# One of sixteen weight transfers of a pair issued from GpSimd's queue instead of SyncE's, in a cross-attention block

## The chip, the cores and the metric

The kernel runs on one core of a Trainium2 chip. The metric is the device time of one execution in microseconds, and less is better. A core has five engines that run side by side and wait for one another by semaphores: TensorE (PE, with PEld for its weight loads), VectorE (DVE), ScalarE (ACT), GpSimd (POOL) and SyncE (SP). Each takes its instructions in the order in which the program issues them. A DMA is issued from the queue of one engine, and its bytes are moved by 16 DMA engines that all queues share. In this kernel nearly all DMAs are issued from SP.

## The reference

A transformer block on 128 sequences of 128 tokens and 256 features, all in float32, with 16 heads of 16 features each and a hidden layer of 1024:

```python
q = (query @ Wq + bq).reshape(b, s, N_HEADS, D_K).transpose(0, 2, 1, 3)
k = (key @ Wk + bk).reshape(b, s, N_HEADS, D_K).transpose(0, 2, 1, 3)
v = (values @ Wv + bv).reshape(b, s, N_HEADS, D_K).transpose(0, 2, 1, 3)
scores = jnp.einsum('bhqd,bhkd->bhqk', q, k) / jnp.sqrt(jnp.float32(D_K))
allowed = j < i + mask                      # mask is 0: strictly earlier tokens
scores = jnp.where(allowed, scores, NEG_INF)
attn = jax.nn.softmax(scores, axis=-1)
attn = attn.at[:, :, 0, :].set(0.0)
ctx = jnp.einsum('bhqk,bhkd->bhqd', attn, v)
ctx = ctx.transpose(0, 2, 1, 3).reshape(b, s, d)
x = layer_norm(query + ctx @ Wo + bo, ln1_g, ln1_b)
ffn = jax.nn.relu(x @ W1 + b1) @ W2 + b2
out = layer_norm(x + ffn, ln2_g, ln2_b)
```

`query` is the input `x`, `key` and `values` are the input `ctx_1024`.

## The kernel before

**Pairs and steps.** Two sequences form a pair, so there are 64 pairs. The schedule is written out by hand: for every engine, the order of the calls in the program is the order in which that engine works. Pairs 0 to 8 and 61 to 63 have their calls written out one by one. In between, `steps(9, 60)` runs one list, `order`, once per step. An entry of that list is a name and a lag, and `ops` says what the name does for which pair, so that one step holds the scores of pair p, the softmax weighting of pair p - 1 (`weigh`, lag -1 on `p - 2`), the hidden layer of pair p - 3 and the second product of pair p - 4.

**What happens to the attention weights.** For pair p the scores come from TensorE (`scores_both`, L502), are masked by VectorE (L516, L974), turned into exponentials by ScalarE (L997) and multiplied by the reciprocal of their sums by GpSimd (`sums`, L557, three calls a pair). VectorE then transposes them within blocks of 32 x 32 (`turn`, L574, three calls a pair), from `sm` into `tb`. The blocks now stand on the wrong partitions. `bring` (L600) carries them to the right ones: 16 DMAs, SBUF to SBUF, one for each row block i and each block column j, from 32 partitions of `tb` to 32 partitions of `pT`, 768 floats on each. `EVERY` is `range(16)`, and `u` = 4 i + j. The DMAs are issued at L608, in four groups of four: `br0`, `br4`, `br8`, `br12` (L1488 to L1491). One step later `weigh` multiplies `pT` with the values (L642, L652). `sm`, `tb` and `pT` rotate through four buffers (`wide`), and the buffer of `pT` for pair p is that of `tb` for pair p - 1.

**The order at the end of a step.** These are the last entries of `order`, with the engine that each one uses:

| Entry | What it issues | Engine |
|---|---|---|
| `sum0` | third `sums` of pair p (L557) | GpSimd |
| `bo` | adds a bias to the tokens (L274) | GpSimd |
| `turn2` | third `turn` of pair p (L574) | VectorE |
| `fin1` | half of the last layer norm of pair p - 5 (L787, L794) | ScalarE, GpSimd |
| `x1g` | scales a residual of pair p - 3 (L761) | GpSimd |
| `x1out` | four DMAs of the first layer norm's result to DRAM (L256) | SP |
| `br0` | four DMAs of `bring` | SP |
| `x1in` | one DMA back from DRAM (L262) | SP |
| `br12`, `br4`, `br8` | twelve DMAs of `bring` | SP |

The next step's first GpSimd instruction is `hs2` (L1025). With `hs0` (L1023), `hs1` (L1027) and `hs3` (L1029) it combines the hidden layer of a pair into `hS`, from which the second product (L1064, `S3` to `S7`) reads. The calls `xs0` to `xs3` (L1110 to L1116) do the same for the hidden layer's input, `xS`, read by L1156. L717 to L724 work out the scale and shift of both layer norms (`sd`, `nb`), which ScalarE reads at L745 and L787.

GpSimd issues no DMA in this kernel.

Of the kernel before, what the change touches and what calls it, by code (L numbers as in the profile page):

```python
# [20 lines left out]
def tile_cross_attention_block(  # L21
# [22 lines left out]
    nc = tc.nc  # L44
# [401 lines left out]
    def wide(name):  # L446
        kind, p = name.split("_")
        turn_ = 3 * (int(p) - 7) + ("sm", "tb", "pT").index(kind)
        at = SOFT[name] if name in SOFT else (2, 3, 1, 0)[turn_ % 4]
        return soft.tile([P, NS * (H + HH) * 32], F32, tag=f"wide{at}", name=name)  # L450
# [149 lines left out]
    def bring(p, queue, which):  # L600

        st = states[p]
        if "pT" not in st:
            pT = st["pT whole"] = wide(f"pT_{p}").rearrange("p (i n) -> p i n", i=NS)
            st["pT"] = pT.rearrange("p i (n a) -> p i n a", a=32)
        for u in which:
            i, j = u // NS, u % NS
            queue.dma_start(  # L608
                st["pT whole"][32 * j : 32 * j + 32, i, :], st["tb"][32 * i : 32 * i + 32, j, :]
            )  # L610
# [665 lines left out]
    EVERY = range(NS * NS)  # L1276
# [81 lines left out]
    def step_tables():  # L1358
# [129 lines left out]
            "br0": lambda p: bring(p, nc.sync, EVERY[0:4]),  # L1488
            "br4": lambda p: bring(p, nc.sync, EVERY[4:8]),
            "br8": lambda p: bring(p, nc.sync, EVERY[8:12]),  # L1490
            "br12": lambda p: bring(p, nc.sync, EVERY[12:16]),  # L1491
        }
        order = (
# [20 lines left out]
        return ops, order  # L1514

    ops, order = step_tables()

    def steps(first, last):
# [1432 lines left out]
```

## Time and profile before

| What | Value |
|---|---|
| Median of two runs | 1477.27 us (1477.25 to 1477.29) |
| Profiled execution, from its first to its last instruction | 1476.5 us |
| Mean granted clock of TensorE | 0.999 |
| DMAs of `bring` (L608), all from SP | 976, of 96 KB each |
| Bytes moved on SP's queue (q1) | 202.49 MB |

A row of a group of instructions names its line, engine, operation and what is written from what is read, then the shapes, the count, the busy time in us, the mean of one in ns, and the idle time of the engine just before them with what ended it. A row of the timeline gives start and length in us. A row of waits gives the sum in us, how often, and the longest. The busy times of a stretch list, for each engine, busy us and the number of instructions, then TensorE's granted clock, the share of the DMA engines that was in use, and GB/s. SPq, POOLq and PEldq are the queues of these engines: DMA issues and semaphore instructions, which the profile does not count as the engine's busy time.

### The profile page before, as it was taken

The numbers are of one execution on the slowest core, as the hardware profiler recorded it, in microseconds if no ns is written. First come the engines' busy times: TensorE is split into PE (matmuls) and PEld (weight loads), VectorE is DVE, ScalarE is ACT, GpSimd is POOL, SyncE is SP. The second block draws the span as 40 slices with busy tenths as digits, with TensorE's granted clock in tenths as the row PEclk, the third lists the DMA queues.
The fourth block names the chain that finished last, engine by engine and source line by source line (L and its number), as shares of the span: only waits on it lengthen the run. The fifth ranks groups of instructions, "written<-read, shape, count | busy, mean of one in ns | idle before, by whom it ended". The sixth has DMA issues, their size and how long they took to land.

```text
span 1476.5 us, 53972 instructions
## 1 busy us (share of the span) xinstructions
PE 1463.9 (99%) x19696; PEld 1377.8 (93%) x19696; DVE 1315.5 (89%) x2897; ACT 1323.0 (90%) x5279; POOL 1388.2 (94%) x1484
## 2 busy tenths in 40 slices
PE   9999999999999999999999999999999999999998
PEld 7788999999999999999999999999999999999998
DVE  7999899999998998998998999989989999999866
ACT  5758999999999999999999999999999999999863
POOL 7788999999999999999999999999999999999987
PEclk9999999999999999999999999999999999999999
DMA  8465566655656666666556566556565666664451
GB/s 203 96 141 127 133 146 139 147 138 136 156 141 138 141 146 139 148 144 145 138 135 154 139 142 141 144 135 157 141 139 136 146 141 150 136 152 122 116 162 58
DMA packets 417865, 206.22 MB, mean 140 GB/s; under 512 B 282434, under 2 KB 386114, under 8 KB 417602
## 3 DMA queue, kind: packets, MB, share of 16 engines
q1 hardware_dynamic: 416080, 202.49, 58.3%
q8 instruction: 159, 2.61, 0.8%
q14 instruction: 106, 0.85, 0.2%
q10 hardware_dynamic: 1520, 0.27, 0.1%
HBM read 71.84 MB, written 34.87 MB: 72 GB/s over the span
## 4 chain that ended last, share of the span: by engine, by line
PE 95%; DVE 1%; POOL 1%; DMA 1%; SPq 1%; issue 1%; ACT 0%; DVEq 0%; POOLq 0%
PE phs L1156 25%; PE pX L1064 11%; PE po L671 7%; PE pk L281 7%; PE pz L1064 7%; PE py L1064 7%; PE pv L411 7%; PE pq L351 6%; PE pss L502 6%; PE pc L652 4%; PE pc L642 3%; PE ph L917 1%; PE pq L281 1%; PE py L940 1%; SPq L608 1%; POOL sm L557 1%
## 5 line engine op out<-in xcount | busy, mean ns | idle before, releaser
L557 POOL TENSOR_TENSOR sm<-sm,rs 128x1024 f32<-128x1024 f32 x192 | 364.0, 1898 | 2.4 <-DVE rs L566 2.3
L997 ACT ACTIVATE sm<-pss,nmx 128x128 f32<-128x128 f32 x944 | 331.9, 395 | 8.4 <-DVE nmx L980 2.4
L997 ACT ACTIVATE sm<-sm,nmx 128x64 f32<-128x64 f32 x944 | 321.4, 361 | 0.8 <-DVE nmx L987 0.2
L1190 ACT ACTIVATE hT<-hT,b1e_c 128x256 f32<-128x256 f32 x480 | 216.1, 501 | 53.9 <-DVE hT L1181 44.7
L574 DVE STREAM_TRANSPOSE tb<-sm 128x1024 f32<-128x1024 f32 x186 | 227.8, 1226 | 1.5 <-POOL sm L557 1.4
L997 ACT ACTIVATION_READ_ACCUMULATOR sm<-pss,nmx 128x1 f32 x912 | 214.7, 235 | 0.0
L997 ACT ACTIVATION_READ_ACCUMULATOR sm<-sm,nmx 128x1 f32 x912 | 193.8, 212 | 0.0
L1156 PE MATMUL phs<-xS,w1t 128*128 128x128 f32 x1440 | 180.2, 275 | 0.0
L1156 PEld LDWEIGHTS phs<-xS,w1t 128*128 128x128 f32 x1440 | 170.4, 192 | 0.0
L980 DVE TENSOR_REDUCE nmx<-pss 128x4 f32<-128x512 f32 x236 | 160.6, 682 | 1.9
L401 ACT ACTIVATE kT<-pk,bkh,half 128x256 f32<-128x256 f32 x252 | 140.0, 559 | 4.1 <-PE pk L281 4.1
L516 DVE TENSOR_TENSOR sm<-pss,neg 128x256 f32<-128x256 f32 (+1 forms) x276 | 113.8, 436 | 16.5 <-PE pss L502 12.5
L1064 PE MATMUL pX<-wt,hS 128*128 128x128 f32 x960 | 126.8, 275 | 0.0
L1156 PE MATMUL phs<-x1T,w 128*128 128x128 f32 x960 | 126.5, 275 | 0.0
L1156 PEld LDWEIGHTS phs<-x1T,w 128*128 128x128 f32 x960 | 120.7, 192 | 3.0
L671 PE MATMUL po<-wo,cxT 128*128 128x256 f32 x512 | 121.8, 381 | 0.0
L411 PE MATMUL pv<-wv,cT 128*128 128x256 f32 x512 | 120.9, 379 | 0.0
L281 PE MATMUL pk<-cT,wk 128*128 128x256 f32 x504 | 119.5, 380 | 0.0
L1064 PEld LDWEIGHTS pX<-wt,hS 128*128 128x128 f32 x960 | 117.0, 192 | 0.1
L411 PEld LDWEIGHTS pv<-wv,cT 128*128 128x128 f32 x512 | 96.9, 190 | 13.1
L671 PEld LDWEIGHTS po<-wo,cxT 128*128 128x128 f32 x512 | 92.5, 190 | 12.2 <-issue 1.6
L281 PEld LDWEIGHTS pk<-cT,wk 128*128 128x128 f32 x504 | 91.5, 190 | 10.5 <-issue 0.2
(192 smaller groups left out, 4149.3 us busy)
## 6 DMA issues: line engine op xcount, KB each, us to landing
pT<-tb SPq DMA_DIRECT2D x976, 96.0 KB, 2.3
x1t<-tbx SPq DMA_DIRECT2D x252, 64.0 KB, 2.7
x1T<-x1t SPq DMA_DIRECT2D x63, 256.0 KB, 3.4
out_dram<-t SPq DMA_DIRECT2D x63, 256.0 KB, 4.3
xb<-in_x_dram SPq DMA_DIRECT2D x124, 128.0 KB, 3.3
cb<-in_ctx_dram SPq DMA_DIRECT2D x124, 128.0 KB, 3.2
x<-in_x_dram SPq DMA_DIRECT2D x31, 512.0 KB, 5.0
w<-in_L_xattn_W_dram SPq DMA_DIRECT2D x2, 1024.0 KB, 7.8
```

Of the source, the lines that this page charges most:

```text
L281: nc.tensor.matmul(ps[:, m * TP : (m + 1) * TP], w[:, k, m * P : (m + 1) * P], src[:, k, :], start=(k == 0), stop=(k == KC - 1),)
L401: nc.scalar.activation(st["kT"][:, m, e, :], pk[:, m * TP : (m + 1) * TP], AF.Identity, bias=bkh[:, m, e : e + 1], scale=half[:, e : e + 1],)
L411: nc.tensor.matmul(pv[:, s * D : (s + 1) * D], st["cT"][:, k, s * P : (s + 1) * P], wv[:, k, :], start=(k == 0), stop=(k == KC - 1),)
L516: nc.vector.tensor_tensor(probabilities(p, hi)[:, 4 * r : 4 * r + 4, :], st["sps", hi][r][:, : 4 * n].rearrange("p (n j) -> p n j", j=n), ...
L557: nc.gpsimd.tensor_tensor(sm[:, part, :], sm[:, part, :], rs[:, :, None].to_broadcast([P, part.stop - part.start, n]), ALU.mult,)
L574: nc.vector.transpose(st["tb"][:, :, at : at + 256].rearrange("p j (n a) -> p n j a", a=32), probabilities(p, hi).rearrange("p h j -> p (h ...
L671: nc.tensor.matmul(po[:, s * D : (s + 1) * D], cxT[:, k, s, :], wo[:, k, :], start=(k == 0), stop=(k == KC - 1),)
L980: nc.vector.tensor_reduce(maxima(p, 1)[:, 4 * r : 4 * r + 4], st["sps", 1][r].rearrange("p (n j) -> p n j", j=P), AX.X, ALU.max, negate=True,)
L997: nc.scalar.activation(sm[:, h, :], src, AF.Exp, bias=nmx[:, h : h + 1], scale=1.0, **({"accum_out": st["su", hi][:, h : h + 1]} if summed ...
L1064: nc.tensor.matmul(out, left(k), right(k), start=(first and k == 0), stop=(k == K - 1), skip_group_check=True,)
L1156: nc.tensor.matmul(ps[:, i * P : (i + 1) * P].rearrange("p (n a) -> p n a", a=32), left(i), right, start=(i == 0 and which not in self.ONT ...
L1190: nc.scalar.activation(self.hT[:, f], self.hT[:, f], AF.Relu, bias=b1e_c[:, f : f + 1], scale=1.0,)
```

## The change

In `br12` the first three transfers (u = 12, 13, 14) go on being issued from SP, and the fourth (u = 15, from partitions 96 to 127 of `tb` to partitions 96 to 127 of `pT`) is issued from GpSimd's queue. `br12` is called through `ops` for pairs 7 to 62. Pairs 2 to 6 call `bring` directly and stay with SP, as does pair 63, which goes by way of DRAM.

```diff
@@ -1488,7 +1488,7 @@
             "br0": lambda p: bring(p, nc.sync, EVERY[0:4]),
             "br4": lambda p: bring(p, nc.sync, EVERY[4:8]),
             "br8": lambda p: bring(p, nc.sync, EVERY[8:12]),
-            "br12": lambda p: bring(p, nc.sync, EVERY[12:16]),
+            "br12": lambda p: (bring(p, nc.sync, EVERY[12:15]), bring(p, nc.gpsimd, EVERY[15:16])),
         }
```

The function that both calls reach is not changed:

```python
for u in which:
    i, j = u // NS, u % NS
    queue.dma_start(
        st["pT whole"][32 * j : 32 * j + 32, i, :], st["tb"][32 * i : 32 * i + 32, j, :]
    )
```

Nothing else in the program differs.

## The prediction

> **What bounds the kernel now.** I read the page first, then the chain that ended last in order of time, then the busy times of single steps, then the waits and the timeline of each engine inside one step.
>
> ```profile
> PE 1463.9 (99%) x19696; PEld 1377.8 (93%) x19696; DVE 1315.5 (89%) x2897; ACT 1323.0 (90%) x5279; POOL 1388.2 (94%) x1484
> PE 95%; DVE 1%; POOL 1%; DMA 1%; SPq 1%; issue 1%; ACT 0%; DVEq 0%; POOLq 0%
> ...
> 808.21 4.47 PE phs L1156 x40
> 830.66 4.47 PE phs L1156 x40
> ```
>
> The first two lines are the page's, the other two the chain's. TensorE carries 95% of the chain, and the same forty matmuls come back after 830.66 - 808.21 = 22.45 us. That is one step, in which every pair of the pipeline advances by one stage. What the other engines have left in a step is told by the busy times of exactly one step:
>
> ```profile
> core 0: us, PE busy (x) PEld busy (x) DVE busy (x) ACT busy (x) POOL busy (x), PEclk, DMA share, GB/s
> 816.54:838.98 22.44, 22.44 (x312) 21.41 (x311) 20.42 (x48) 21.24 (x89) 21.65 (x23) 1.00 0.65 153
> ```
>
> TensorE is full, at a granted clock of 1.00. GpSimd (POOL) is busy 21.65 us of 22.44. So it is the runner-up, with 0.79 us free at most, and most of that is not free either, as its timeline shows around the place of the change:
>
> ```profile
> 810.71 1.90 POOL L557 TENSOR_TENSOR sm<-sm,rs 128x1024 f32<-128x1024 f32 x1
> 812.57 1.30 POOL L274 TENSOR_TENSOR xb<-x,bov_r 128x512 f32<-128x512 f32 x1
> 813.82 1.30 POOL L794 TENSOR_TENSOR t<-t,g_r 128x512 f32<-128x512 f32 x1
> 815.08 1.27 POOL L761 TENSOR_TENSOR t<-t,g_r 128x512 f32<-128x512 f32 x1
> 816.54 1.27 POOL L1025 TENSOR_TENSOR hS<-hT 128x512 f32<-128x512 f32 x1 [0.19 <-ACT hT L1190]
> ...
> 821.45 1.27 POOL L1027 TENSOR_TENSOR hS<-hS,hT 128x512 f32<-128x512 f32 x1
> 822.80 1.27 POOL L1029 TENSOR_TENSOR hS<-hT,hS 128x512 f32<-128x512 f32 x1
> ```
>
> Each instruction starts as the one before it ends. The exceptions are gaps of about 0.08 us before an instruction that reads its predecessor's result (L1029 after L1027, 822.80 - 822.72), which stay whatever happens, and one wait for ScalarE before L1025. The waits of GpSimd from 200 to 1340 us say how much it waits for others:
>
> ```profile
> POOL hS L1025 <- ACT hT L1190: 8.9, 50, 0.2
> POOL sd L717 <- DVE mv L1318: 1.7, 11, 0.2
> ```
>
> 8.9 / 50 = 0.18 us of true slack a step (the second row adds 0.03, and I leave it). GpSimd could run a step in 22.45 - 0.18 = 22.27 us. It is a second bound, 0.8% behind the first.
>
> **What the change does, part by part.** `br12` (L1491) is called for pairs 7 to 62, which are 56 pairs. Of its four transfers the last (u = 15: row block 3 to partitions 96 to 127, 96 KB) goes to GpSimd's queue. The transfers of pairs 2 to 6 and 63 are as before.
>
> *Taken from SyncE (SP): one issue a pair.*
>
> ```profile
> L608 SPq DMA_DIRECT2D pT<-tb x976: 507/591/2024, 55.7 to 1409.1; - x196
> ...
> DMA to landing us min/median/max: 2.0/2.3/5.5
> ...
> SPq L256 <- DVE tbx L882: 209.1, 58, 7.1
> 815.03 1.51 SPq L608 DMA_DIRECT2D pT<-tb  x1
> ...
> 819.12 8.42 SPq L608 DMA_DIRECT2D pT<-tb  x12
> ```
>
> The issue takes 591 ns (median). SP waits 209.1 / 58 = 3.6 us a step for VectorE's `tbx`, so 0.59 us less on it makes its idle longer and no more. Nor is an earlier landing worth anything. SP's last issue of the step ends at 819.12 + 8.42 = 827.54 and lands within 5.5 us, at 833.0, and the reader of these weights (`weigh`, L642) starts one step after this row:
>
> ```profile
> 812.61 0.43 PE L642 MATMUL pc<-pT,vd 128*32 128x64 f32 x16
> 813.63 1.23 DVE L574 STREAM_TRANSPOSE tb<-sm 128x1024 f32<-128x1024 f32 x1
> 824.02 1.06 PE L1064 MATMUL pX<-wt,hS 128*128 128x128 f32 x8
> ```
>
> That is at 812.61 + 22.45 = 835.06. This part I cost at nothing. Its cover is at least 2 us before the weigh and 3.6 us of idle SP.
>
> *Put on GpSimd: one issue a pair, between L761 (`x1g`) and L1025 (`hs2` of the next step).* Does it wait there? It needs the transposed weights: VectorE's L574 ends at 813.63 + 1.23 = 814.86, and GpSimd reaches the issue at 815.08 + 1.27 = 816.35, so the data has been there for 1.5 us. It also needs the old content of its target buffer read, the weights `tb` of the pair before. SP needs the same and issues from 815.03. So there is no wait, and nothing is queued up by one. The transfer itself would land by 816.35 + 2 + 5.5 = 823.9 even with a slow issue, 11 us ahead of the weigh.
>
> What remains is the time for which the issue keeps GpSimd from L1025, and the trace of before shows no DMA issued by GpSimd. Rows near it, groups of instructions with the mean in ns (those of L717 to L557 from 200 to 1340 us, the others of the whole span):
>
> ```profile
> L140 POOL MEMSET power<- 128x4 f32 x1 | 0.1, 101 | 0.3 <-POOLq L2932 0.3
> ...
> L717 POOL TENSOR_TENSOR sd<-mv,eps 128x4 f32<-128x4 f32 x51 | 10.3, 202 | 7.3 <-DVE mv L1318 1.7
> L718 POOL TENSOR_TENSOR sd<-sd,power 128x4 f32<-128x4 f32 x51 | 51.9, 1017 | 4.0
> L1029 POOL TENSOR_TENSOR hS<-hT,hS 128x512 f32<-128x512 f32 x51 | 65.0, 1274 | 4.0
> L557 POOL TENSOR_TENSOR sm<-sm,rs 128x1024 f32<-128x1024 f32 x152 | 288.4, 1897 | 0.0
> ...
> L1181 DVE TENSOR_TENSOR hT<-hT,phs 128x512 f32<-128x512 f32 x60 | 41.3, 689 | 11.1 <-PE phs L1156 10.7
> ```
>
> From below, the price is the shortest thing that GpSimd does, 0.10 us, which fits into the 0.18 us of slack. A gain is excluded, since GpSimd is only given work and SP's saving falls into idle time. From above, it is 1.90 us, GpSimd's longest instruction (SP's own longest issue of such a transfer, 2.02 us, lies close). Between these ends I take the same issue's 0.591 us on SP, times the ratio by which GpSimd is slower than another engine at a like piece of work, L1029 against VectorE's L1181: 1274 / 689 = 1.85. That is 1.09 us, an estimate. The row nearest to it points the same way: the power of four columns takes 1.02 us where an addition of the same shape takes 0.20, so an instruction that makes GpSimd work through something longer costs about a microsecond at almost no data.
>
> The Trainium skill, in "DMA: Bandwidth & Descriptors", section Specifications, gives about 1 µs to the first byte of a DMA from GpSimd, and about 0.6 µs for one from the sync queue. The second agrees with the 591 ns of the SP row here; the first no row of this trace can show. With 1.0 us for the issue the sum below would end at 1522 us.
>
> *What this does to the step.* GpSimd's step becomes 22.27 + 1.09 = 23.36 us, and TensorE's stays 22.45. GpSimd is then the bound, and falls back by 1.09 - 0.18 = 0.91 us a step until TensorE waits for it. The first of its results that TensorE misses is `hs1` (L1027, ended at 821.45 + 1.27 = 822.72), read by the matmuls at 824.02: 1.30 us of cover, used up in the second step. ScalarE feels it at once:
>
> ```profile
> ACT hT L1190 <- DVE hT L1181: 38.9, 51, 0.8
> ACT t L745 <- POOL nb L724: 18.5, 51, 0.4
> ```
>
> It already waits 18.5 / 51 = 0.36 us a step for GpSimd's `nb`, but has another 38.9 / 51 = 0.76 us of waiting ahead of the relus, and with a longer step more.
>
> *Taking the transfer on a second queue.* `weigh` has one more semaphore to look at. The nearest row for that is TensorE's own:
>
> ```profile
> L1064 PEldq EVENT_SEMAPHORE  x128: 51/51/51, 144.3 to 1461.1; - x128
> ```
>
> At worst that is 56 x 0.051 = 2.9 us. TensorE, no longer the bound, has 0.9 us a step in which it vanishes, so I count nothing. If GpSimd did not become the bound, it would be on the path.
>
> **The sum.** 56 x 0.91 = 51.0 us, less the 1.3 us of cover, is +49.7 us. The profiled execution spans 1476.5 us and the median of the two runs is 1477.27, 0.8 more. 1476.5 + 49.7 + 0.8 = 1527.0 us, which is 3.4% more.
>
> **The rivals.**
>
> *GpSimd's queue issues while its engine computes (no change).* The issue would pass beside L761's 1.27 us, as SP's issues pass beside everything. Then 0.18 us of slack is never exceeded and the time is 1477, or 1480 with the extra semaphore on TensorE. For it: a DMA issue is not an elementwise instruction, and no row shows one holding up GpSimd's engine. Against it: none shows one that doesn't, and GpSimd takes its instructions in order. The Trainium skill speaks on both sides. "DMA: Bandwidth & Descriptors", section Issuing engines are not separate DMA queues, says that issuing from several engines only saves the issuing sequencer's time, by which this change would be nearly free; "GPSIMD Engine Reference", section 4, says that the descriptors of such a DMA are made by two of GpSimd's own cores, by which it is not. No run so far shows either. Chance 10%, and another 4% for an issue that does hold the engine but costs less than SP's 0.59 us: 1477 to 1499.
>
> *A heavier issue, or a wait at it.* If the issue takes longer than 1.90 us, or has to wait on GpSimd for something that came before SP's issues, every instruction behind it waits too. SP's first issue of this step took 1.51 us where the median is 0.59, so some transfers are slow to leave. At 2.5 us: 56 x (2.5 - 0.18) - 1.3 = +129, 1606 us. Against it: the data is there 1.5 us early, and the buffer is free when SP starts. Chance 5%.
>
> *Faster.* It would take a wait of TensorE that goes. TensorE idles 1476.5 - 1463.9 = 12.6 us in all, 0.9% of the span, none of it for these weights in the steady steps. Chance 1%.
>
> **How the numbers follow.** The forecast, that GpSimd's issue costs between 0.59 and 1.90 us and GpSimd sets the step, has 80%. At 0.59 us the time is 56 x 0.41 - 1.3 = +21.7, 1499 us; at 1.90 us it is 56 x 1.72 - 1.3 = +95, 1572 us. This is the range, with 15% left out below and 5% above. The line of 2%, which is about what a measurement of this kernel can tell from no change, is at +29.5 us, an issue of (29.5 + 1.3) / 56 + 0.18 = 0.73 us. I give 6% to the stretch from 0.59 to 0.73 us. Slower by over 2%: 80 - 6 + 5 = 79%. Within 2%: 10 + 4 + 6 = 20%. Faster: 1%.
>
> **What would show it.** In the profile after: 56 issues of L608 on GpSimd's queue, and between L761 and L1025 a stretch of about 1.1 us where 0.19 us stood. The steps in the chain 23.36 us apart instead of 22.45. The wait of L1025 for ScalarE gone. TensorE waiting for `hS` or `xS` by about 0.9 us a step, and GpSimd in the chain. If the steps stay at 22.45, the issue is beside the engine's work; if they are longer than 23.4 and GpSimd still stands still ahead of the issue, it is a wait; if they are longer with GpSimd standing elsewhere, a loop through other engines set the pace and my sum by GpSimd alone was wrong.

## The result, and the profile after

The changed kernel takes 1493.53 us (median of two runs, 1492.06 to 1495.01) against 1477.27 us before. The ratio is 1.011, with a 95% interval of 1.0081 to 1.0140. It is slower by 1.1%. That is the direction of the forecast and a third of its size, and it lies under the low end of the range, 1499.

The profiled execution spans 1493.0 us, 16.5 more than that of before. On the page, the busy times and the queue of GpSimd's DMAs read as follows:

```profile
PE 1475.0 (99%) x19696; PEld 1380.5 (92%) x19696; DVE 1314.6 (88%) x2897; ACT 1325.0 (89%) x5279; POOL 1415.9 (95%) x1540
...
q0 software_dynamic: 1792, 5.51, 1.6%
...
pT<-tb POOLq DMA_DIRECT2D x56, 96.0 KB, 2.7
```

GpSimd has 56 instructions more (1540 against 1484), though only DMA issues were added to it. So the issues count as work of the engine itself, which the issues of SP do not. GpSimd's busy time grows by 1415.9 - 1388.2 = 27.7 us. The transfers land 2.7 us after the issue.

The timeline of GpSimd over the same place of a step shows the issue in its row, and the next step's L1025:

```profile
813.84 0.46 POOL L1116 TENSOR_TENSOR xS<-x1T,xS 128x128 f32<-128x128 f32 x1
814.26 0.20 POOL L717 TENSOR_TENSOR sd<-mv,eps 128x4 f32<-128x4 f32 x1
...
822.20 1.29 POOL L761 TENSOR_TENSOR t<-t,g_r 128x512 f32<-128x512 f32 x1
823.43 0.58 POOL L608 DMA_DIRECT2D pT<-tb  x1
824.04 1.28 POOL L1025 TENSOR_TENSOR hS<-hT 128x512 f32<-128x512 f32 x1
...
846.66 1.28 POOL L1025 TENSOR_TENSOR hS<-hT 128x512 f32<-128x512 f32 x1
```

The issue starts as L761 ends, takes 0.58 us, and moves L1025 to 824.04 - 823.43 = 0.61 us after its start. There is no wait ahead of L608, and L1025 no longer waits for ScalarE. The step is 846.66 - 824.04 = 22.62 us, 0.17 more than before, not 0.91 more.

The starts of L1025 also divide the 16.5 us by where they arise. The first one stands at 147.76 us before and at 149.27 after; the last one, 59 starts later, at 1458.48 and at 1472.91:

| Stretch | Before | After | Difference |
|---|---|---|---|
| Start of the span to the first L1025 | 147.76 | 149.27 | +1.5 |
| First to last L1025 | 1310.72 | 1323.64 | +12.9 |
| Last L1025 to the end | 18.02 | 20.09 | +2.1 |

56 steps at 0.18 us make 10, less than the 12.9 of the middle row. The rest shows in the later steps. These are the starts of L1025 from GpSimd's timeline between 1180 and 1310 us:

```profile
1187.28 1.28 POOL L1025 TENSOR_TENSOR hS<-hT 128x512 f32<-128x512 f32 x1
1210.43 1.28 POOL L1025 TENSOR_TENSOR hS<-hT 128x512 f32<-128x512 f32 x1
1233.06 1.28 POOL L1025 TENSOR_TENSOR hS<-hT 128x512 f32<-128x512 f32 x1
1256.19 1.28 POOL L1025 TENSOR_TENSOR hS<-hT 128x512 f32<-128x512 f32 x1
1278.84 1.28 POOL L1025 TENSOR_TENSOR hS<-hT 128x512 f32<-128x512 f32 x1
1302.11 1.28 POOL L1025 TENSOR_TENSOR hS<-hT 128x512 f32<-128x512 f32 x1
```

The distances are 23.15, 22.63, 23.13, 22.65 and 23.27 us: every second step is half a microsecond longer. Up to about 600 us all were 22.6 to 22.7; after that about every fourth is longer by 0.1 to 0.3, and from about 1140 us on every second one as here. The waits from 200 to 1340 us, and TensorE's timeline at one of the long steps, say where it stops:

```profile
ACT t L745 <- POOL nb L724: 37.7, 50, 1.1
DVE tb L574 <- POOL sm L557: 22.0, 39, 1.0
...
ACT hT L1190 <- DVE hT L1181: 20.6, 50, 0.8
...
PEld pss L502 <- issue: 8.6, 13, 1.0
PE pss L502 <- issue: 3.4, 9, 0.7
```

```profile
1230.05 1.12 PE L502 MATMUL pss<-kT,qT 32*64 32x128 f32 x34
1231.41 1.09 PE L502 MATMUL pss<-kT,qT 32*64 32x256 f32 x30 [0.24 <-issue]
```

The first two rows of the waits are GpSimd's lag, felt by the others: ScalarE waits 37.7 / 50 = 0.75 us a step for `nb` where it was 0.36, and VectorE's transposes now wait for `sums`. The last two rows are something else. TensorE stops in the midst of the 64 matmuls of the scores, and the profile names no releaser. The two rows, of its weight loads and of its matmuls, are largely the same stops. No such row stands among the waits of before. The third thing is at the very end, in the drain of GpSimd's queue (L2946; the three numbers are shortest, median and longest in ns). The first row is of before, the second of after:

```profile
L2946 POOLq DRAIN  x3: 39/78/651, 1472.5 to 1476.2; - x3
```

```profile
L2946 POOLq DRAIN  x3: 34/102/5244, 1487.0 to 1492.7; - x3
```

### The profile page after: what moved, and what is told of

Same layout as the page of the kernel before. It is cut to its first block, busy times and chain, and to the rows that moved or that the text cites. A ratio compares the mean times of both kernels' runs of the same rounds, so it can differ in the third digit from the quotient of the medians.

```text
span 1493.0 us, 54034 instructions
## 1 busy us (share of the span) xinstructions
PE 1475.0 (99%) x19696; PEld 1380.5 (92%) x19696; DVE 1314.6 (88%) x2897; ACT 1325.0 (89%) x5279; POOL 1415.9 (95%) x1540
## 5 line engine op out<-in xcount | busy, mean ns | idle before, releaser
L1190 ACT ACTIVATE hT<-hT,b1e_c 128x256 f32<-128x256 f32 x480 | 216.0, 501 | 36.0 <-DVE hT L1181 27.5
L997 ACT ACTIVATION_READ_ACCUMULATOR sm<-sm,nmx 128x1 f32 x912 | 190.7, 209 | 0.0
L1156 PE MATMUL phs<-xS,w1t 128*128 128x128 f32 x1440 | 180.8, 276 | 0.0
L1156 PEld LDWEIGHTS phs<-xS,w1t 128*128 128x128 f32 x1440 | 170.3, 192 | 0.1
L516 DVE TENSOR_TENSOR sm<-pss,neg 128x256 f32<-128x256 f32 (+1 forms) x276 | 113.9, 436 | 27.1 <-PE pss L502 23.1
L1156 PE MATMUL phs<-x1T,w 128*128 128x128 f32 x960 | 126.5, 275 | 0.0
L1156 PEld LDWEIGHTS phs<-x1T,w 128*128 128x128 f32 x960 | 120.9, 192 | 2.8
L671 PE MATMUL po<-wo,cxT 128*128 128x256 f32 x512 | 121.8, 381 | 0.0
L745 ACT ACTIVATE t<-t,nb,sd 128x256 f32<-128x256 f32 x126 | 69.4, 594 | 47.3 <-POOL nb L724 45.3
L502 PE MATMUL pss<-kT,qT 32*64 32x256 f32 (+1 forms) x3840 | 103.7, 331 | 3.6 <-issue 3.4
```

Of the source, the lines that this page charges most:

```text
L516: nc.vector.tensor_tensor(probabilities(p, hi)[:, 4 * r : 4 * r + 4, :], st["sps", hi][r][:, : 4 * n].rearrange("p (n j) -> p n j", j=n), ...
L671: nc.tensor.matmul(po[:, s * D : (s + 1) * D], cxT[:, k, s, :], wo[:, k, :], start=(k == 0), stop=(k == KC - 1),)
L997: nc.scalar.activation(sm[:, h, :], src, AF.Exp, bias=nmx[:, h : h + 1], scale=1.0, **({"accum_out": st["su", hi][:, h : h + 1]} if summed ...
L1156: nc.tensor.matmul(ps[:, i * P : (i + 1) * P].rearrange("p (n a) -> p n a", a=32), left(i), right, start=(i == 0 and which not in self.ONT ...
L1190: nc.scalar.activation(self.hT[:, f], self.hT[:, f], AF.Relu, bias=b1e_c[:, f : f + 1], scale=1.0,)
```

## The experiments

Three causes were in question: GpSimd's time for the issue, the stops of TensorE, and the drain. Each run was compared with runs of the kernel before on the same chip (medians 1476.68, 1476.94 and 1476.84 us).

The stops of TensorE need one fact. In a step of before, TensorE's queue holds exactly 640 instructions: 310 weight loads, 310 matmuls, semaphore instructions, and six empty ones which `Second(p - 4, 6)` adds. After the change it holds 639, since the number of semaphore instructions fell. The first row is of before, the second of after (instructions of the weighing, L642):

```profile
L642 PEldq EVENT_SEMAPHORE  x315: 51/51/2114, 64.9 to 1432.9; - x158
```

```profile
L642 PEldq EVENT_SEMAPHORE  x263: 51/51/1685, 66.4 to 1448.1; - x132
```

That matters if TensorE's instructions come in blocks. The page of before lists a queue for them:

```profile
q8 instruction: 159, 2.61, 0.8%
```

159 packets of 2.61 MB are 16.4 KB each, and 2.61 MB over the 40,655 instructions that the trace has for TensorE's queue are 64 bytes each: a packet is a block of 256 instructions, and 640 are two and a half blocks. At 640 a step the ends of the blocks stand at the same five places of every two steps. At 639 they move by one instruction a step. The theory was that a block whose end falls in the scores comes too late. The rival was that the stops are a consequence of GpSimd's lag.

### Filled up to 640 again (e1_pe640)

```diff
-        return once("second", p - 4, lambda: Second(p - 4, 6))
+        return once("second", p - 4, lambda: Second(p - 4, 7))
```

> The changed kernel with one more empty instruction a step on TensorE (7 pads instead of 6), so that its queue again holds 640 instructions a step as before the change, where the change had left 639. Theory T (two losses: GpSimd's step is 22.63 us, and TensorE's instruction fetch slips by one instruction a step until it stalls in the scores every second step): the stalls at L502 go, all steps are 22.62 to 22.64 us apart, 56 x 0.19 = 10.6 us over before, about 1488 us. Rival R (everything comes from the transfer on GpSimd's queue, TensorE's count has no part): 1492 to 1495 us as the changed kernel, with the stalls at L502 where they were.

On the kernel after. Measured: 1490.06 us (1488.85 to 1490.48), ratio 1.0088 (1.0073 to 1.0103). All steps of the middle are 22.61 to 22.66 us, and no stop in L502 is left. From the first to the last L1025 it takes 1320.18 us: 9.5 more than before, and 3.5 less than after. GpSimd's share of the loss is thus 9.5 us, that of the stops 3.5.

The profile lists no wait of TensorE for GpSimd in these steps. Where TensorE loses its 0.19 us a step is read from its starts:

```profile
832.34 0.47 POOL L1114 TENSOR_TENSOR xS<-xS,x1T 128x128 f32<-128x128 f32 x1
832.43 1.25 DVE L574 STREAM_TRANSPOSE tb<-sm 128x1024 f32<-128x1024 f32 x1 [0.81 <-POOL sm L557]
832.86 0.97 PEld L1156 LDWEIGHTS phs<-xS,w1t 128*128 128x128 f32 x8
832.92 1.10 PE L1156 MATMUL phs<-xS,w1t 128*128 128x128 f32 x8
833.60 0.25 DVE L1088 TENSOR_TENSOR t<-t,py 128x128 f32<-128x128 f32 x1
833.90 1.16 PE L1064 MATMUL py<-w,hS 128*128 128x128 f32 x8
```

The next block of TensorE starts at 834.90. From start to start these two blocks of eight matmuls take 0.98 and 1.00 us, where in the kernel before they take 0.90 and 0.89 (827.81, 828.71, 829.60). The first follows the end of GpSimd's `xS` (L1114, 832.81) by 0.05 us. The second follows VectorE's reading of `py` (L1088, 833.85) by 0.05 us, and VectorE is late there since its transpose waited 0.81 us for GpSimd's `sums`.

### 639 in the kernel before (e2_before639)

```diff
-        return once("second", p - 4, lambda: Second(p - 4, 6))
+        return once("second", p - 4, lambda: Second(p - 4, 5))
```

> The kernel before, all sixteen transfers on SP, with 5 pads instead of 6, so that TensorE's queue holds 639 instructions a step. Theory T: the slip alone, without GpSimd's issue. The first 15 to 20 steps of the loop stay at 22.45 us, after that every second step is longer by 0.5 to 1.0 us with an idle TensorE at L502; in all +8 to +16 us, 1485 to 1493 us. Rival R: one empty instruction less changes nothing, 1477 us.

On the kernel before, all DMAs on SP. Measured: 1490.77 us (1489.52 to 1497.71), ratio 1.0104 (1.008 to 1.0127). One empty instruction fewer a step costs 14.1 us, nearly as much as the change under study. Up to about 590 us the steps are 22.4 us; then longer ones of 23.1 to 23.9 come in, and from about 955 us on nearly every second one is long. Its waits from 200 to 1340 us:

```profile
PEld pss L502 <- issue: 10.2, 13, 1.3
...
PE pss L502 <- issue: 4.4, 7, 1.0
```

The second row is of the same stops as the first, so the two are not added. The 50 steps from the fourth to the 54th start of L1025 take 12.0 us more than before, in 14 long steps, which is most of the loss of 14.1. The rival falls: GpSimd does nothing new here. In the kernel after, the weight loads' row has 8.6 us and yet the stops cost only 3.5. An explanation, not tested by itself, is that with GpSimd setting the step TensorE has 0.18 us a step to spare, and a stop comes out of that first.

### The blocks moved once (e3_shift40, e7_shift76)

```diff
+    empty(40)
     steps(9, 60)
```

> The changed kernel, 639 instructions a step as it is, with 40 empty instructions once on TensorE ahead of the loop over steps 9 to 60 (40 x 0.013 = 0.5 us). Theory T: the slip now runs from +40 to -12 instead of from 0 to -52, and never reaches the place at about -15 where the stalls began; steps of 22.63 us to the end, about 1488 us. Rival R: 1492 to 1495 us with the stalls where they were.

Forty empty instructions in TensorE's queue, once, ahead of the steady steps of the kernel after. They were to keep the slip out of the scores until the end. They did not. Measured: 1499.7 us (1498.94 to 1501.11), ratio 1.0155 (1.0138 to 1.0172). Every second step is long from the first on, and later, when the slip of one a step has carried the blocks back to within some ten instructions of their old place, the steps are 22.6 again. So the place is bad on both sides, and it isn't the slip that costs but the place. To test that, the other number was put into the kernel before, at 640 a step:

```diff
+    empty(76)
     steps(9, 60)
```

> The kernel before, 640 instructions a step and all transfers on SP, with 76 empty instructions once on TensorE ahead of the loop (76 x 0.013 = 1 us). Two and a half fetches of 256 instructions make a step, so +76 stands where the changed kernel's slip of -52 ends. Theory T (the place of the fetch in the step decides): from the first steps of the loop to the last, every second step is longer by 0.5 to 1.2 us, +15 to +30 us in all, 1492 to 1507 us. If only a slip, and not a place, did harm: 1478 us.

Measured: 1510.23 us (1507.04 to 1515.36), ratio 1.0228 (1.0206 to 1.0251): 76 empty instructions in the whole program cost 33 us, more than was expected. Every second step is long from first to last. The waits from 200 to 1340 us, and one stop in TensorE's timeline:

```profile
PEld pss L502 <- issue: 22.3, 24, 1.7
...
PE pss L502 <- issue: 10.8, 17, 1.2
```

```profile
1041.03 1.12 PE L502 MATMUL pss<-kT,qT 32*64 32x128 f32 x37
1042.82 1.07 PE L502 MATMUL pss<-kT,qT 32*64 32x256 f32 x27 [0.67 <-issue]
```

Again the rows overlap and are not added. In the 50 steps from the fourth to the 54th start of L1025, where nothing but the place of the blocks differs, the kernel takes 26 us more than before, 1.8% of its time. Another 6.5 us arise ahead of them, mostly in one stop of 5.4 us at 190 us, in the first scores behind the empty instructions; its cause is open. That TensorE waits for the block itself rests on two things. Counted through the traces, the instruction with which TensorE goes on is in all 13 stops of the kernel after, 13 of e2 and 24 of this one number 193 or 194 of 256, counted from 0 (from 200 to 1340 us), so the stops stand whole blocks apart, whatever the step. And the last bytes of the block, among the packets of the instruction queue, stand at a nearly fixed distance ahead of TensorE's going on:

```
run            last byte of the block   TensorE goes on   distance
e7_shift76     1041.35                  1042.82           1.47
after          1229.99                  1231.41           1.42
after          1275.82                  1277.33           1.51
e2_before639   1226.85                  1228.29           1.44
e2_before639   1272.38                  1273.86           1.48
e3_shift40      303.34                   304.90           1.56
e3_shift40      349.52                   350.98           1.46
```

Over all stops of these kernels the distance is 1.2 to 1.6 us, and TensorE enters no block sooner after its last byte; in the kernel before, which has no such stop, the least distance is 1.65 and the median 7.9. Why the scores are a bad place was not tried; in e3 five of the stops lie in L351 and L671 instead, at the same place of a block. What their rows show is how dense they are: 64 matmuls, each with its weight load, in 1.6 us.

### GpSimd's time without a DMA (e5_memsets)

```diff
+    idle = const.tile([P, P], F32, tag="idle", name="idle")
...
-            "br12": lambda p: bring(p, nc.sync, EVERY[12:16]),
+            "br12": lambda p: (bring(p, nc.sync, EVERY[12:16]), [nc.gpsimd.memset(idle, 0.0) for _ in range(3)]),
```

> No transfer is moved: all sixteen on SP as before, 640 instructions a step on TensorE. In the place of the moved issue GpSimd fills a scratch tile of 128 columns three times, which nothing reads (a 128x128 fill takes about 0.20 us). Theory T (the issue costs what it keeps GpSimd busy): GpSimd's step is 22.02 + 0.5 to 0.6 = 22.5 to 22.6 us, +0.08 to 0.17 us a step, 1481 to 1486 us, with no long drain at the end. Rival (the cost comes with the DMA, by its second queue or its semaphores, not from GpSimd's time): 1477 us.

On the kernel before: three fills of a tile that nobody reads, in the place of the issue, all DMAs left on SP. GpSimd's timeline:

```profile
823.57 0.73 POOL L1492 MEMSET idle<- 128x128 f32 x3
824.27 1.27 POOL L1026 TENSOR_TENSOR hS<-hT 128x512 f32<-128x512 f32 x1
...
846.98 1.27 POOL L1026 TENSOR_TENSOR hS<-hT 128x512 f32<-128x512 f32 x1
```

The fills hold GpSimd for 824.27 - 823.57 = 0.70 us, more than the 0.5 to 0.6 wanted, and the step is 22.71. Measured: 1490.94 us (1490.0 to 1491.9), ratio 1.0095 (1.008 to 1.011), where 1481 to 1486 was expected. The step is the reading that counts: 22.71 - 0.70 and 22.63 - 0.61 both leave about 22.01 us for GpSimd's other work. So it is the time for which GpSimd is held that matters, whatever holds it, and its true slack was 22.44 - 22.02 = 0.42 us a step.

### Less other work for GpSimd (e6_less_pool)

```diff
-        nc.gpsimd.tensor_tensor(nb, nb, minus[:, :n], ALU.mult)
...
-        return once("second", p - 4, lambda: Second(p - 4, 6))
+        return once("second", p - 4, lambda: Second(p - 4, 7))
```

> The kernel of e1 (one transfer on GpSimd, 640 instructions a step) without the multiplication of nb by -1 on GpSimd (L724), so the outputs differ; it takes GpSimd 0.28 us a step with the gap before it. Theory T: GpSimd's step becomes 22.63 - 0.28 = 22.35 us, less than TensorE's 22.45, so steps are 22.45 us again although the issue is still on GpSimd; what stays over before is the drain at the end, about 2 us: 1479 us. If the transfer cost something by another way than GpSimd's time: 1486 to 1490 us.

On the kernel after, at 640 a step. It leaves out the multiplication of `nb` by -1, so it does not compute the reference's function. Measured: 1479.38 us (1478.89 to 1482.06), ratio 1.0019 (1.0009 to 1.0028). The first seven steps of the loop take 22.36 us, all later ones are back at 22.45, with the DMA still on GpSimd. So the transfer on another queue costs the steps nothing by itself, only GpSimd's time does. What remains of the loss is 2.4 us, and the drain is still 5.244 us long.

### Two transfers on GpSimd, and half the pairs (e4_two_on_pool, e8_half)

```diff
-            "br12": lambda p: (bring(p, nc.sync, EVERY[12:15]), bring(p, nc.gpsimd, EVERY[15:16])),
+            "br12": lambda p: (bring(p, nc.sync, EVERY[12:14]), bring(p, nc.gpsimd, EVERY[14:16])),
```

> Two of the sixteen transfers (u = 14 and 15) from GpSimd's queue, and 5 pads, so that TensorE holds 640 instructions a step. If each issue holds GpSimd for 0.61 us and GpSimd's step without one is 22.02 us: 22.02 + 1.22 = 23.24 us a step, +0.79 x 56 = +44 us, about 1521 us. If an issue's cost is mostly a fixed one for using the second queue at all: about 1488 us as with one.

On the kernel after, with five empty instructions in `Second`, which makes 640. Measured: 1521.28 us (1520.94 to 1523.91), ratio 1.0304 (1.0289 to 1.032). The total is that of the expectation, but not by its terms. GpSimd's timeline and the drain:

```profile
811.04 1.28 POOL L761 TENSOR_TENSOR t<-t,g_r 128x512 f32<-128x512 f32 x1
812.26 1.08 POOL L608 DMA_DIRECT2D pT<-tb  x2
813.36 1.29 POOL L1025 TENSOR_TENSOR hS<-hT 128x512 f32<-128x512 f32 x1
```

```profile
L2946 POOLq DRAIN  x3: 34/102/9817, 1509.3 to 1519.6; - x3
```

Two issues hold GpSimd for 1.10 us, so the second adds 0.49, not 0.61, and the steps are 23.12 instead of 23.24. The drain of 9.8 us makes up for it. In this kernel the waits of TensorE's weight loads that the prediction named do appear, from 200 to 1340 us:

```profile
PEld pX L1064 <- POOL hS L1027: 8.7, 40, 0.2
...
PEld phs L1156 <- POOL xS L1114: 7.4, 45, 0.2
```

The other kernel issues from GpSimd for pairs 7 to 34 only:

```diff
+            "br12": lambda p: (bring(p, nc.sync, EVERY[12:15]), bring(p, nc.gpsimd if p < 35 else nc.sync, EVERY[15:16])),
...
+        return once("second", p - 4, lambda: Second(p - 4, 7 if p < 36 else 6))
```

> The transfer from GpSimd's queue for pairs 7 to 34 only (28 instead of 56), from SP for the rest, with 7 pads as long as TensorE's count needs it and 6 after. Steps of 22.63 us up to pair 34 and 22.45 us after, +28 x 0.18 = +5 us. GpSimd's drain at the end, 5.24 us after 56 transfers and 9.82 us after 112, is 0.66 + 28 x 0.082 = 2.95 us if it grows with their count, which ends beside SP's last wait: 1482 us in all. If the drain is the same for any count, it is 5.2 us and the time 1484 us.

Measured: 1480.06 us (1479.25 to 1481.46), ratio 1.0023 (1.0013 to 1.0032). The steps are 22.6 us while GpSimd issues and 22.45 afterwards. The two steps in between take 22.04 and 22.08 us: GpSimd, late by then, catches up at the pace of its own work, which agrees with the 22.02 found above. The drain is 2.957 us. Side by side, with the distance from the last L1025 to the end of the span:

| Kernel | DMAs from GpSimd | Drain, us | Last L1025 to end, us |
|---|---|---|---|
| before | 0 | 0.651 | 18.02 |
| e8_half | 28 | 2.957 | 18.0 |
| after | 56 | 5.244 | 20.1 |
| e4_two_on_pool | 112 | 9.817 | 24.7 |

The drain grows by (9.817 - 0.651) / 112 = 0.082 us for each DMA that GpSimd ever issued. The first 3.2 us of it pass beside other work (5.24 - 2.07, and 9.82 - 6.65). What exceeds that is added to the end: 2.1 us here.

### The same transfer from ScalarE's queue (e9_scalar_queue)

```diff
-            "br12": lambda p: (bring(p, nc.sync, EVERY[12:15]), bring(p, nc.gpsimd, EVERY[15:16])),
+            "br12": lambda p: (bring(p, nc.sync, EVERY[12:15]), bring(p, nc.scalar, EVERY[15:16])),
```

> The same transfer from ScalarE's queue instead of GpSimd's, with 640 instructions a step on TensorE (7 pads). ScalarE has 0.76 + 0.36 = 1.12 us of waiting in a step of 22.45, and no long drain is expected. If an issue holds it for about the 0.59 us that SP takes and that fits into these waits: steps of 22.45 us, 1477 to 1479 us. If an issue on any engine with work behind it costs a step its full length, or the delayed exponentials hold up GpSimd's sums (0.42 us of slack there): up to 22.6 us a step, 1479 to 1487 us.

On the kernel after, at 640 a step. The timeline of ScalarE around the issue:

```profile
818.91 0.51 ACT L1190 ACTIVATE hT<-hT,b1e_c 128x256 f32<-128x256 f32 x1
819.04 0.51 ACTq L608 DMA_DIRECT2D pT<-tb  x1
819.32 1.69 ACT L1190 ACTIVATE hT<-hT,b1e_c 128x256 f32<-128x256 f32 x4
```

The issue, 819.04 to 819.55, lies beside ScalarE's own work: the next L1190 starts 0.41 us after the one ahead, where 0.40 is usual. The drain is the 0.651 us of before. Still it is no gain: 1488.85 us (1484.82 to 1492.59), ratio 1.009 (1.0071 to 1.0108), where at most 1487 was expected. The steps are irregular, 22.4 to 23.6. TensorE's stops, from 200 to 1340 us, lie at the hidden layer:

```profile
PE phs L1156 <- DMA x1T<-x1t: 1.3, 5, 0.4
```

```profile
PEld phs L1156 <- issue: 11.1, 30, 0.8
```

The transfer of `x1T` itself lands in 3.3 us as before, but it is issued later. SP's waits, from 200 to 1340 us, have a row that the kernel before has not:

```profile
SPq L608 <- DMA pT<-tb: 46.8, 48, 2.5
```

Nearly once a step SP stands still ahead of one of the transfers of `br0` until ScalarE's transfer, issued just before, has landed. In the step shown that is at 821.64, and SP issues at 821.66. The issue of `x1T` (L262) stands behind it in SP's queue and comes about 1 us later. So `x1T` lands 0.11 us (median) ahead of the first weight load of L1156 that reads it, where it was 0.81 in the kernel before, and TensorE's stops end 0.1 us after that landing (600.70 and 600.80, 691.26 and 691.36, 804.62 and 804.72). Why SP waits for ScalarE's transfer, and not for GpSimd's in the kernel after, isn't settled.

## Why the prediction was right and wrong

**Right.** GpSimd became the bound; it has no wait at the issue; SP's 0.59 us was worth nothing; L1025's wait for ScalarE went; the 56 issues stand where they were said to, and the time went up. The rival by which the issue passes beside the engine's work is refuted on GpSimd (e5 and e6) and true of ScalarE's queue (e9). Two of the signs did not come: TensorE has no listed wait for `hS` or `xS` in the kernel after, and GpSimd is not in the chain, which the profile after follows over 6% of the span only. The result that TensorE misses first is not `hs1`, with 1.30 us of cover, but `xS` (L1114) and, by way of VectorE, `sums`, as e1 shows. The time lies in the stretch from 1477 to 1499 us that was given to an issue of less than 0.59 us; that is by chance, since the issue takes 0.61 and what was larger is the slack. The Trainium skill, in "DMA: Bandwidth & Descriptors", section Issuing engines are not separate DMA queues, speaks of the sequencer's time only; on GpSimd the 0.58 us is time of the engine, and 9.5 of the 16.5 us come from it.

**The price of the issue: 1.09 us, measured 0.61.** This term was mis-sized. "The ratio by which GpSimd is slower than another engine at a like piece of work" was taken from additions of 128 x 512 numbers, and an issue adds no numbers. The row of the same instruction on SP, 0.591 us, used as the low end, came nearest. The Trainium skill's 1 µs in that page's Specifications, set into the sum as if it were this price, is a latency to the first byte, and so is its 0.6 µs for the sync queue, whose agreement with SP's 591 ns, the length of an issue, therefore says nothing. The nearest thing that the runs show is the landing, 2.7 us from GpSimd against 2.3 from SP in the kernel after, but 2.4 from both in e6.

**The slack: 0.18 us, measured 0.42.** This step broke the range. Two things were missed, and both stood in the quoted rows. Instructions of GpSimd that follow each other start about 0.04 us before the recorded end of the one ahead (813.82 after 812.57 + 1.30), so the wait at L1025 was not 0.18 but 816.54 - (815.08 + 1.27 - 0.04) = 0.23 us. And the wait of L717 was left out at 0.03 us a step. The waits name a releaser for only 1.7 us of it, but the group's row has 7.3 us of idle time before 51 instructions, and the timeline of before shows a gap at that place:

```profile
806.54 0.45 POOL L1116 TENSOR_TENSOR xS<-x1T,xS 128x128 f32<-128x128 f32 x1
807.14 0.20 POOL L717 TENSOR_TENSOR sd<-mv,eps 128x4 f32<-128x4 f32 x1
```

From start to start this is 0.60 us where the kernel after needs 814.26 - 813.84 = 0.42. Idle time without a named releaser was taken for a fixed latency, and 0.18 us of it was slack. With both, GpSimd's step is 22.45 - 0.23 - 0.18 + 0.61 = 22.65, against the 22.62 to 22.66 measured. The trace of before has a step that shows the slack directly: at the start of the loop the third L1025 is followed by the fourth after 22.06 us, and at this place e1 and e5 have 22.63 and 22.73, the steps of their GpSimd. The prediction's own low end, an issue of 0.59 us, would have been 56 x (0.59 - 0.42) - 1.3 = +8.2, or 1485.5 us, and the range would have held the result, though the result also holds the stops and the drain, which the sum did not have.

**With the right sizes** the sum's form holds: 56 x (0.61 - 0.42) - 1.3 = +9.3 us, against the 9.5 of e1_pe640. In the trace it is 50 steps at 0.19 us rather than 56 less the cover, so that they agree so closely is in part chance.

**The semaphore, "so I count nothing".** The step said that `weigh` has one more to look at. It had fewer instructions (263 instead of 315), and the effect was not their 0.051 us but the count of TensorE's queue, 639 instead of 640: 3.5 us, shown by e1 and, in the kernel before, by e2. No rival had it.

**The end of the program** was not looked at. Each DMA that GpSimd issued lengthens its drain: 2.1 us on the path.

**Around the span.** The 0.8 us between span and median joined two executions. In executions of before that list both, the time is 1.7 us above the span (1476.22 beside 1474.5), so the profiled execution of before was itself a long one. This changes the forecast by about a microsecond. The 1.5 us at the start of the profiled execution after, before the first GpSimd issue, are absent in the profiled executions of e1 to e7 and e9, and e8 has 1.2 of them. I count them as a variation between executions, which wasn't tested further.

Altogether 9.5 + 3.5 + 2.1 + 1.5 = 16.6 us, against the 16.5 between the two profiles. The terms were read from these profiles and that of e1, so the sum had to come out. They hold to a microsecond or two: the executions of before alone range from 1474.9 to 1479.2, and e1's loss is 13.4 us by the medians and 11.6 by the profiles. No version that was run beats the kernel before. GpSimd is 0.42 us from the bound, less than one issue, and with the queue that does not hold its engine (e9) SP came to wait instead.

## What to carry to other kernels

Moving a DMA issue to GpSimd gives the engine itself 0.6 us of work, so it must fit into GpSimd's slack; find that slack from start to start in the timeline and count idle time that has no named releaser, not only the waits that have one. For an unknown price, look first at the row of the same instruction on another engine; here it came nearer than a scaled one, in this one case. And where TensorE is full, count the instructions of its queue per step before and after an edit, since one empty instruction fewer a step cost 1% here.

## What the runs showed of the hardware

- 76 empty instructions on TensorE, once, made 1477 us into 1510 (ratio 1.0228, 1.0206 to 1.0251). Of this 26 us come from the place at which TensorE's instruction blocks end. TensorE went on 1.2 to 1.6 us after a block's last byte. The Trainium skill, in "Runtime: NRT & Kernel Launch", section Instruction fetch mechanics, has the blocks of 256 instructions, as the trace does, and calls the cost of crossing them mostly hidden; here it is hidden at one place of the step and not at another.
- GpSimd's issue of a 96 KB transfer holds its engine for 0.61 us, and a second one right behind it for 0.49. ScalarE's takes 0.51 us beside the engine's work.
- GpSimd's drain at the end grows by 0.082 us for each DMA that it issued, from 0.65 us for none to 9.82 for 112.
